# Two images through attention and a 3x3: the order at the seams and in the first image's last stage

## Chip, cores and metric

The kernel runs on one core of a Trainium2 chip. The metric is device time in microseconds (us), of which the medians of runs are compared. The engines are PE (matrix products), ACT (one-input functions, also reads products back from the accumulators), DVE (element-wise work and reductions), POOL (element-wise work, slower, and issues some DMAs) and SP (issues DMAs).

## The reference, cut to what matters

Two images of 256 channels and 64x64 pixels go through two layers. Both begin with a group normalisation and add their result to their input.

```python
# layer 0: x = x + attention(_gn(x)), 8 heads over all 4096 pixels
# layer 1: x = x + layer(_gn(x)):
q = _c1x1(x, conv1_w, conv1_b)
k = _c1x1(x, conv2_w, conv2_b)
v = _c1x1(x, conv3_w, conv3_b)
...
ctx = _sa(blockify(fq), blockify(fk), blockify(v), oh, ow)
feats = _bn_relu(_c1x1(ctx, lr_W_w), lr_W_scale, lr_W_shift)
feats = feats.reshape(b, DH, DW, C, oh, ow).transpose(0, 4, 5, 3, 1, 2).reshape(b * oh * ow, C, DH, DW)
qx = _bn_relu(_c1x1(_bn_relu(_c1x1(feats, sr_fq1_w), sr_fq1_scale, sr_fq1_shift), sr_fq2_w), sr_fq2_scale, sr_fq2_shift)
kx = _bn_relu(_c1x1(_bn_relu(_c1x1(feats, sr_fk1_w), sr_fk1_scale, sr_fk1_shift), sr_fk2_w), sr_fk2_scale, sr_fk2_shift)
vx = _c1x1(feats, sr_fv_w)
ctx2 = _sa(qx, kx, vx, DH, DW)
feats2 = _bn_relu(_c1x1(ctx2, sr_W_w), sr_W_scale, sr_W_shift)
out_att = feats2.reshape(b, oh, ow, C, DH, DW).transpose(0, 3, 1, 4, 2, 5).reshape(b, C, h, w)
...
f_all = jnp.einsum('bidn,oi->bodn', jnp.concatenate([qh, kh, vh], 1), fc_w)
f_conv = f_all.transpose(0, 2, 1, 3).reshape(b, hd * KC * KC, h, w)
out_conv = lax.conv_general_dilated(f_conv, dep_w, (1, 1), ((1, 1), (1, 1)), feature_group_count=hd, dimension_numbers=('NCHW', 'OIHW', 'NCHW'))
return rate1 * out_att + rate2 * out_conv
```

`_sa` is a softmax attention over 64 positions, once for each group of 64 pixels: first over pixels eight apart ("lr" in the kernel), then inside 8x8 blocks ("sr"). The last lines are linear in x, so the kernel computes them as one 3x3 convolution of the normalised picture, 256 to 256 channels, whose weights it works out on the chip from `conv1_w` to `conv3_w`, `fc_w` and `dep_w`.

## The kernel before

An image is eight tiles of 512 pixels (`NT` is 8), two partitions' worth of channels each (`KC` is 2): `xts[0]` to `xts[7]`. The loop over the two images `b` runs four stages one after the other.

- *Layer 0's start*: `group_stats` (bn_stats L326, bn_aggr L330, then `pm_l` L333 and `pv_l` L343, two tiny products that sum over a group's channels, with copies and a reciprocal on DVE and a root on ACT, L334 to L363, between and behind them), `normalise` (L368), and `project0`, whose first products are `p_wk` (L418).
- *Layer 0's attention* (to L652): from about 158 to 1150 us for image 0 and 1700 to 2745 us for image 1. Its sum is written back into the tiles (`put`, L652).
- *layer1_first* (from L1089). The seam: `to_groups(k, t, engine)` copies channel half k of tile t, normalised, into `xg` in another pixel order (L1102 on ACT, L1105 on DVE or POOL); `project(t, m, chunks)` multiplies `xg` into `py` (L1136), adds a position term (L1140, which reads `loc`, loaded by `open_pair` L1118) and copies it out (L1141). `st.means` and `st.variances` are `pm_l` and `pv_l` here. In image 0 a generator, `fold_products`, is stepped by `next(fold)` between these: it folds weights together on PE and copies them on ACT (`pt_fv` L263, `pm_fv` L269, `pb_lr` L278, copies L264 and L272, and L283 and L284 on DVE). Eight "lr" tiles of `group_attention` follow.
- *layer1_second* (from L1238): eight "sr" tiles, interleaved with the 3x3. A tile has a query branch (`branch`: `phq_sr` L1281, `prq_sr` L1289), a key branch (`phk_sr`, `prk_sr`), and `group_attention` in three parts: first values (`pvs_sr` L1013) and scores (`sp_sr` L1031) with a softmax on DVE and ACT (`nm_sr` L1045, `e_sr` L1047 and L1048, `den_sr` L1050 and L1051, `e_sr` L1052); then its transposition (`at_sr` L1057) and the other values; then `pc_sr` (L1075), read by ACT into `res`.

The 3x3 is sixteen steps, two tiles of the image (a strip) and a quarter of the work each, four steps to a strip. The picture `xp` is the normalised image with a border, made by `to_image(t)` on ACT (L1249, two instructions a tile). `conv_transform` turns it into `v` on POOL (one `col` L936, four `v` L940); the step ahead is always transformed. `conv_step` multiplies `v` and the weights `wf` (`mm` L950, 32 matmuls), and ACT (L955) and DVE (L956 to L977) add the result onto `xts`. `conv_edges` corrects the border (L984). When the four steps of a strip are done, its two tiles are finished: DVE adds `res` and `xts` (L1332), and SP writes the output (L1335).

For image 0 only, `conv_weights` makes the 3x3's weights on DVE from four loads, in two halves: 108 multiply-adds each (L870, L872), rows (L876 to L878), columns (L881 to L883), and SP writes them to a DRAM tile (L885). That takes DVE through the lr tiles and sr tile 0. `fetch_conv_weights` reads them back (L900, 4 MB); for image 0, PE transposes them (L909, 64 of them), ACT and DVE copy the results (L912, L914), and they are stored for image 1 (L915).

What sets the order: in the seam of layer1_first, PE, ACT and DVE run in the order of the text; in layer1_second only PE does, while a scheduler orders ACT, DVE and POOL from dependences, costs and priorities. SP issues its DMAs in order. In layer1_second the list `steps` says how many 3x3 steps a tile has: the first comes after the query branch, the second after the first part of the attention, the third after its end. Input tiles live in nine buffers, so the second image's tiles x_1_6 and x_1_7 are loaded (`load_x`, L70) only when outputs 5 and 6 of image 0 no longer need their inputs. The col buffer is one; `w4`, which holds `v` and most other intermediate tiles, has eleven.

Of the kernel before, what the change touches and what calls it, by code (L numbers as in the profile page):

```python
# [21 lines left out]
NT = N // T  # L22
KC = C // P
# [17 lines left out]
def direct_layers(ctx: ExitStack, tc: tile.TileContext, a: dict, out: bass.AP, bad: bass.AP):  # L41
# [3 lines left out]
    nc = tc.nc  # L45
# [1045 lines left out]
    def layer1_first(b, xts, put, check, st):  # L1091
# [6 lines left out]
        def to_groups(k, t, eng):  # L1098
            dst = xg[:, k, :, t, :].rearrange("p (d e) o -> p d e o", d=8)
            src = xts[t][:, k, :].rearrange("p (d o e) -> p d e o", d=8, o=8)  # L1100
            if eng is nc.scalar:
                return nc.scalar.activation(  # L1102
                    dst, src, AF.Identity, bias=shift[:, k : k + 1], scale=rstd[:, k : k + 1]
                )
            return eng.tensor_scalar(dst, src, mean[:, k : k + 1], rstd[:, k : k + 1], ALU.subtract, ALU.mult)  # L1105
# [10 lines left out]
        def open_pair(i):  # L1116
            loc = w4([16, 2, T], f"loc_{b}_{i}", F32R)
            nc.sync.dma_start(  # L1118
                out=loc.bitcast(F32).rearrange("r s n -> r (s n)"),
                in_=loc_kept[:, :, :, 2 * i * T : (2 * i + 2) * T].rearrange("l d r n -> (l d r) n"),  # L1120
            )
            locs[i] = loc
# [40 lines left out]
        with tc.manual_schedule(engines={E.PE, E.Activation, E.DVE}):  # L1163
            st.aggregate(second)
            fold = fold_products() if b == 0 else iter(())
            put(nc.gpsimd.tensor_copy, (0, 1))
            for t in range(5, NT):
                to_groups(0, t, nc.gpsimd)
            pm, pv = bank([P, 1], f"pm_l1_{b}"), bank([P, 1], f"pv_l1_{b}")
            to_groups(0, 0, nc.scalar)  # L1170
            next(fold, None)
            to_groups(0, 1, nc.scalar)
            next(fold, None)
            st.means(second, pm, nc.vector.tensor_copy)
            st.spread(second)
            to_groups(0, 2, nc.scalar)
            if b == 1:
                to_groups(0, 3, nc.scalar)
            next(fold, None)
            st.variances(second, pv)  # L1180
            st.deviations(second, pv)
            shift_of(st, 1)
            for _ in range(2):
                next(fold, None)
            for t in range(3 + b, 5):
                to_groups(0, t, nc.scalar)
            put(nc.scalar.copy, (2, 3))
            n_act = 2
            for t in range(NT):
                done = to_groups(1, t, nc.scalar if t < n_act else nc.vector)  # L1190
            for _ in fold:
                pass
            check()
            for i in range(2):
                open_pair(i)
            for t in range(2):
                for m in range(KC):
                    project(t, m, slice(0, 1))
            for t in range(2):
                for m in range(KC):  # L1200
                    project(t, m, slice(1, KC))
            at_grid(0)
        with tc.manual_schedule(engines={E.PE}):

            before = None
            for t in range(NT + 1):
                parts = None
                if t < NT:
                    def to_feats(m, pc, t=t):
# [6 lines left out]
                    parts = group_attention(  # L1216
                        f"lr_{b}_{t}", tiles.pop(t), source(t),
                        lambda c, w, t=t: source(t)[:, c, w * P : (w + 1) * P], wts["w3"], to_feats, b == 0,
                        more=(ats[rows, t // 4, :], grid[rows, :], t == 0),
                    )  # L1220
# [18 lines left out]
    def layer1_second(b, xts, feats, mean, rstd, shift, pacc):  # L1239

        xp = apool.tile([P, KC, PADW, PADW], F32, tag="A", name=f"xp_{b}")
        for k in range(KC):
            nc.gpsimd.memset(xp[:, k, 0, :], 0.0)
            nc.gpsimd.memset(xp[:, k, PADW - 1, :], 0.0)
            nc.gpsimd.memset(xp[:, k, 1 : PADW - 1, 0 : PADW : PADW - 1], 0.0)

        def to_image(t):
            for k in range(KC):
                nc.scalar.activation(  # L1249
                    xp[:, k, 1 + 8 * t : 9 + 8 * t, 1 : 1 + W], xts[t][:, k, :].rearrange("p (r w) -> p r w", w=W),  # L1250
                    AF.Identity, bias=shift[:, k : k + 1], scale=rstd[:, k : k + 1],
                )

        for t in range(3):
            to_image(t)
        results = {}
        turns = [divmod(n, 4) for n in range(4 * NT // 2)]
        ahead = {0: conv_transform(b, xp, *turns[0])}
        done = 0

        steps = (0, 0, 2, 3, 3, 3, 3, 2) if b == 0 else (3, 3, 2, 2, 2, 2, 2, 0)

        def conv():
            nonlocal done
            if done + 1 < len(turns):
                ahead[done + 1] = conv_transform(b, xp, *turns[done + 1])
            conv_step(b, xts, wf, ahead.pop(done), *turns[done], pacc)
            done += 1

        for t in range(NT):  # L1270
            nt = f"sr_{b}_{t}"
            f = [
                feats[k][:, 8 * t : 8 * t + 8].rearrange("p o d e -> p (o d e)") for k in range(KC)
            ]

            def branch(one, two, col1, col2, nm):
                hid = w4([P, KC, T], f"h{nm}_{nt}")
                for m in range(KC):
                    ph = bank([P, T], f"ph{nm}_{nt}_{m}")
                    for k in range(KC):  # L1280
                        nc.tensor.matmul(  # L1281
                            ph, wts[one][:, k, m * P : (m + 1) * P], f[k], start=k == 0, stop=k == KC - 1
                        )
                    bn_relu(hid[:, m, :], ph, col1, m)
                res = w4([P, KC, T], f"r{nm}_{nt}")
                pr = [bank([P, T], f"pr{nm}_{nt}_{m}") for m in range(KC)]
                for k in range(KC):
                    for m in range(KC):
                        nc.tensor.matmul(  # L1289
                            pr[m], wts[two][:, k, m * P : (m + 1) * P], hid[:, k, :], start=k == 0, stop=k == KC - 1  # L1290
                        )
                for m in range(KC):
                    bn_relu(res[:, m, :], pr[m], col2, m)
                return res

            with tc.manual_schedule(engines={mybir.EngineType.PE}):
                q = branch("fq1", "fq2", V_FQ1, V_FQ2, "q")
                for tt in {0: (3, 4)}.get(t, (t + 4,)):
                    if tt < NT:
                        to_image(tt)  # L1300
                if t == sum(n == 0 for n in steps[:-1]):
                    wf = fetch_conv_weights(b)
                if steps[t] > 0:
                    conv()
                k = branch("fk1", "fk2", V_FK1, V_FK2, "k")
                res = w4([P, KC, T], f"res_{nt}")

                def to_res(m, pc, res=res):

                    bn_relu(  # L1310
                        res[:, m, :].rearrange("p (d o e) -> p o d e", d=8, o=8),
                        pc.rearrange("p (o d e) -> p o d e", o=8, d=8), V_SRW, m,
                    )

                parts = group_attention(
                    nt, q, k, lambda c, w, f=f: f[c][:, w * P : (w + 1) * P], wts["fv"], to_res, apart=t + 1 < NT
                )
                next(parts)
                if steps[t] > 1:
                    conv()  # L1320
                next(parts)
                next(parts, None)
                if steps[t] > 2:
                    conv()
            conv_edges(xts, t)
            if b == B - 1 and t == 2:
                report()
            results[t] = res
            for n in sorted(n for n in results if done >= 4 * (n // 2 + 1)):
                res = results.pop(n)  # L1330
                for m in range(KC):
                    nc.vector.scalar_tensor_tensor(  # L1332
                        res[:, m, :], res[:, m, :], wts["rate1"], xts[n][:, m, :], ALU.mult, ALU.add
                    )
                nc.sync.dma_start(  # L1335
                    out=out[b, :, n * T : (n + 1) * T].rearrange("(k p) n -> p k n", p=P), in_=res
                )


    for b in range(B):  # L1340
        xts = x_first if b == 0 else load_x(b)
# [14 lines left out]
        with tc.tile_pool(name=f"sc_{b}", bufs=1, space=PSUM) as psum["sc"]:  # L1356
            put, check, st = attention0(b, xts, held)
# [565 lines left out]
```

## Time and profile before

| what | us |
|---|---|
| three runs | 3169.22, 3171.24, 3173.57 (median 3171.24) |
| profiled execution, its own time | 3168.58 |
| its span from first to last instruction | 3166.8 |
| mean granted TensorE clock | 0.989 |
| PE busy in the span | 3056.7 |
| DVE, ACT, POOL busy | 2467.7, 2304.5, 856.5 |

The profiled execution lies inside the runs' spread. A span of 3166.8 us with 1.8 us around it makes the execution's 3168.58. The page gives the span in 40 slices of 79 us: the digits are tenths of busy time, and in the row PEclk tenths of full clock. A row of a timeline has the start in us, the length in us, the engine, the line of the code, what is computed from what, how many such instructions it groups, and in brackets how long the engine stood idle before and what ended that. A row of windows has the stretch's limits and length, then busy time and number of instructions of PE, weight loads, DVE, ACT and POOL, the granted clock, the share of DMA time and GB/s. Image 0's stages of layer 1 lie from 1150 to 1600 us, image 1's from 2745 us to the end.

### The profile page before, as it was taken

The numbers are of one execution on the slowest core, as the hardware profiler recorded it, in microseconds if no ns is written. First come the engines' busy times: TensorE is split into PE (matmuls) and PEld (weight loads), VectorE is DVE, ScalarE is ACT, GpSimd is POOL, SyncE is SP. The second block draws the span as 40 slices with busy tenths as digits, with TensorE's granted clock in tenths as the row PEclk, the third lists the DMA queues.
The fourth block names the chain that finished last, engine by engine and source line by source line (L and its number), as shares of the span: only waits on it lengthen the run. The fifth ranks groups of instructions, "written<-read, shape, count | busy, mean of one in ns | idle before, by whom it ended". The sixth has DMA issues, their size and how long they took to land. (4 is left out here: it accounts for less than half of the span.)

```text
span 3166.8 us, 62680 instructions
## 1 busy us (share of the span) xinstructions
PE 3056.7 (97%) x25107; PEld 1832.7 (58%) x25107; DVE 2467.7 (78%) x3204; ACT 2304.5 (73%) x2359; POOL 856.5 (27%) x929
## 2 busy tenths in 40 slices
PE   7999999999999999799979999999999999899998
PEld 4455555555555546467755555555555555466766
DVE  4599999999999988745645999889999999824543
ACT  2699999999999973432225999999999999734232
POOL 2122222222222230435400222222222222305530
PEclk9999999999999999899989999999999999999999
DMA  7968779678796651211149696786878965600000
GB/s 249 276 127 171 152 160 182 135 171 171 162 191 127 140 127 52 83 54 54 40 163 276 131 185 141 154 175 144 171 168 164 186 145 125 161 1 8 21 14 22
DMA packets 242709, 425.74 MB, mean 134 GB/s; under 512 B 99164, under 2 KB 109984, under 8 KB 239976
## 3 DMA queue, kind: packets, MB, share of 16 engines
q0 software_dynamic: 96240, 240.41, 38.0%
q1 hardware_dynamic: 146168, 181.24, 20.3%
q8 instruction: 199, 3.26, 0.4%
q14 instruction: 102, 0.84, 0.1%
HBM read 118.52 MB, written 68.12 MB: 59 GB/s over the span
## 5 line engine op out<-in xcount | busy, mean ns | idle before, releaser
L564 DVE TENSOR_TENSOR e<-e,es 128x1024 f32<-128x1024 f32 (+1 forms) x952 | 1035.7, 1142 | 93.7 <-ACT es L517 91.7
L527 PE MATMUL av<-es,v 128*32 128x256 f32 (+1 forms) x9644 | 746.4, 390 | 0.0
L564 DVE TENSOR_TENSOR e<-e,v 128x1024 f32<-128x1024 f32 (+1 forms) x640 | 676.4, 1108 | 55.4 <-ACT v L517 54.0
L517 ACT ACTIVATE es<-sa 128x1536 f32<-128x1536 f32 (+1 forms) x444 | 635.9, 1432 | 95.3 <-PE sa L511 52.6
L511 PE MATMUL sa<-q,k 128*128 128x512 f32 x1736 | 560.9, 430 | 13.8 <-ACT es L517 6.6
L527 PE MATMUL av<-v 128*32 128x256 f32 (+1 forms) x6228 | 507.1, 390 | 0.0
L527 PEld LDWEIGHTS av<-es,v 128*32 128x32 f32 x9644 | 316.2, 109 | 299.5 <-issue 161.0
L511 PEld LDWEIGHTS sa<-q,k 128*128 128x128 f32 x1736 | 280.0, 188 | 296.0 <-issue 138.5
L511 PE MATMUL sc<-q,k 128*128 128x512 f32 x1180 | 371.5, 396 | 3.2 <-ACT es L517 2.1
L511 PE MATMUL sb<-q,k 128*128 128x512 f32 x1180 | 371.0, 395 | 0.0
L527 PEld LDWEIGHTS av<-v 128*32 128x32 f32 x6228 | 216.8, 110 | 179.2 <-issue 82.1
L517 ACT ACTIVATE es<-sc 128x1024 f32<-128x1024 f32 x296 | 306.4, 1035 | 1.7 <-DMA v<-es 1.7
L517 ACT ACTIVATE v<-sc 128x1024 f32<-128x1024 f32 x294 | 304.4, 1035 | 0.0
L517 ACT ACTIVATE es<-sb 128x1024 f32<-128x1024 f32 x296 | 302.0, 1020 | 0.7 <-DMA acc<-es 0.6
L517 ACT ACTIVATE v<-sb 128x1024 f32<-128x1024 f32 x294 | 300.0, 1020 | 0.0
L511 PEld LDWEIGHTS sc<-q,k 128*128 128x128 f32 x1180 | 210.0, 188 | 74.4 <-ACT es L517 13.5
L511 PEld LDWEIGHTS sb<-q,k 128*128 128x128 f32 x1180 | 221.2, 188 | 54.1 <-ACT es L517 1.6
L574 POOL DMA_DIRECT2D es<-es x118 | 100.7, 854 | 500.9 <-ACT es L517 436.6
L517 ACT ACTIVATE v<-sa 128x1536 f32<-128x1536 f32 (+1 forms) x146 | 209.3, 1434 | 35.5 <-PE sa L511 15.0
L950 PE MATMUL mm<-v,wf 128*128 128x256 f32 x1024 | 227.5, 380 | 0.0
L940 POOL TENSOR_TENSOR v<-col 128x512 f32<-128x512 f32 x128 | 161.5, 1289 | 238.8 <-PE mm L950 81.0
L950 PEld LDWEIGHTS mm<-v,wf 128*128 128x128 f32 x1024 | 193.5, 190 | 34.2 <-issue 8.6
(259 smaller groups left out, 3222.6 us busy)
## 6 DMA issues: line engine op xcount, KB each, us to landing
acc<-es POOLq DMA_DIRECT2D x130, 512.0 KB, 6.1
acc<-v POOLq DMA_DIRECT2D x84, 512.0 KB, 6.0
es<-es POOLq DMA_DIRECT2D x138, 256.0 KB, 4.1
v<-es POOLq DMA_DIRECT2D x134, 256.0 KB, 4.9
k<-wk_halves SPq DMA_DIRECT2D x64, 512.0 KB
q<-wq_halves SPq DMA_DIRECT2D x256, 128.0 KB
v<-v POOLq DMA_DIRECT2D x90, 256.0 KB, 4.8
es<-v POOLq DMA_DIRECT2D x86, 256.0 KB, 3.9
```

The source lines that it names most:

```text
L511: nc.tensor.matmul(sc[:, i, :], held["k", g // 2][:, j * P : (j + 1) * P], held["q", g, u // 2][:, u % 2, :], start=True, stop=True,)
L517: nc.scalar.activation(dst, sc[:, i : i + m, :], AF.Exp, scale=SC0)
L527: nc.tensor.matmul(dst[HD0 * u : HD0 * u + HD0, n], lhs, rhs(u)[:, n], start=start, stop=stop)
L564: nc.vector.tensor_add(dst[:, s, :], dst[:, s, :], src)
L574: nc.gpsimd.dma_start(out=dst, in_=src, accum_op=ALU.add)
L940: (nc.gpsimd.tensor_add if plus else nc.gpsimd.tensor_sub)(dst, rows(one), rows(two))
L950: nc.tensor.matmul(mm[:, m, r, :], wf[:, k, 4 * r + q, m * P : (m + 1) * P], v[r // 2][:, r % 2, k, :], start=k == 0, stop=k == KC - 1,)
```

## The change

At the seam into layer1_first, for both images: `open_pair` comes first; of the five copies of tiles 0 to 4 of the first channel half, which are ACT's, four (image 0) or five (image 1) now stand ahead of the means; image 0's folding pieces stand between them; x_6's and x_7's copies are given to POOL; in image 1 ACT takes three instead of two of the second half's copies, and one `project` half is issued between means and variances.

In layer1_second of image 0: steps (0, 0, 2, 3, 3, 3, 3, 2) become one in tile 1, after its first attention part, three in each of tiles 2 to 6, and none in tile 7. `to_image` and the first `conv_transform` are written in tiles 1 to 3 instead of ahead of the loop. The weights are fetched at the first step, in tile 1 after its scores, instead of in tile 2 after the query branch. Tile 0's second and third attention parts are kept back (`pending`) and issued after tile 1's query branch. The edges of tiles 0 and 1 are both added after tile 1. In image 1, `spots` and `images` give the same steps as before.

```diff
--- before.py
+++ after.py
@@ -1167,35 +1167,34 @@
             for t in range(5, NT):
                 to_groups(0, t, nc.gpsimd)
             pm, pv = bank([P, 1], f"pm_l1_{b}"), bank([P, 1], f"pv_l1_{b}")
-            to_groups(0, 0, nc.scalar)
-            next(fold, None)
-            to_groups(0, 1, nc.scalar)
-            next(fold, None)
+            for i in range(2):
+                open_pair(i)
+            for t in range(3):
+                to_groups(0, t, nc.scalar)
+                next(fold, None)
+            to_groups(0, 3, nc.scalar)
+            if b:
+                to_groups(0, 4, nc.scalar)
             st.means(second, pm, nc.vector.tensor_copy)
             st.spread(second)
-            to_groups(0, 2, nc.scalar)
-            if b == 1:
-                to_groups(0, 3, nc.scalar)
+            firsts = [lambda t=t, m=m: project(t, m, slice(0, 1)) for t in range(2) for m in range(KC)]
+            if b:
+                firsts.pop(0)()
             next(fold, None)
             st.variances(second, pv)
             st.deviations(second, pv)
             shift_of(st, 1)
-            for _ in range(2):
-                next(fold, None)
-            for t in range(3 + b, 5):
-                to_groups(0, t, nc.scalar)
-            put(nc.scalar.copy, (2, 3))
-            n_act = 2
+            if b == 0:
+                to_groups(0, 4, nc.scalar)
+            put(nc.gpsimd.tensor_copy, (2, 3))
+            n_act = 2 + b
             for t in range(NT):
                 done = to_groups(1, t, nc.scalar if t < n_act else nc.vector)
             for _ in fold:
                 pass
             check()
-            for i in range(2):
-                open_pair(i)
-            for t in range(2):
-                for m in range(KC):
-                    project(t, m, slice(0, 1))
+            for first in firsts:
+                first()
             for t in range(2):
                 for m in range(KC):
                     project(t, m, slice(1, KC))
@@ -1251,22 +1250,32 @@
                     AF.Identity, bias=shift[:, k : k + 1], scale=rstd[:, k : k + 1],
                 )
 
-        for t in range(3):
-            to_image(t)
         results = {}
         turns = [divmod(n, 4) for n in range(4 * NT // 2)]
-        ahead = {0: conv_transform(b, xp, *turns[0])}
+        ahead = {}
         done = 0
-
-        steps = (0, 0, 2, 3, 3, 3, 3, 2) if b == 0 else (3, 3, 2, 2, 2, 2, 2, 0)
+        wf = None
+
+
+        spots = {t: (0, 1, 2) for t in range(2, 7)} | {1: (1,)} if b == 0 else {
+            t: (0, 1, 2) if t < 2 else (0, 1) for t in range(NT - 1)
+        }
+        images = {1: range(5), 2: (5, 6), 3: (7,)} if b == 0 else {0: (3, 4), 1: (5,), 2: (6,), 3: (7,)}
 
         def conv():
-            nonlocal done
+            nonlocal done, wf
+            if wf is None:
+                wf = fetch_conv_weights(b)
             if done + 1 < len(turns):
                 ahead[done + 1] = conv_transform(b, xp, *turns[done + 1])
             conv_step(b, xts, wf, ahead.pop(done), *turns[done], pacc)
             done += 1
 
+        if b:
+            for t in range(3):
+                to_image(t)
+            ahead[0] = conv_transform(b, xp, *turns[0])
+        pending = None
         for t in range(NT):
             nt = f"sr_{b}_{t}"
             f = [
@@ -1295,12 +1304,15 @@
 
             with tc.manual_schedule(engines={mybir.EngineType.PE}):
                 q = branch("fq1", "fq2", V_FQ1, V_FQ2, "q")
-                for tt in {0: (3, 4)}.get(t, (t + 4,)):
-                    if tt < NT:
-                        to_image(tt)
-                if t == sum(n == 0 for n in steps[:-1]):
-                    wf = fetch_conv_weights(b)
-                if steps[t] > 0:
+                if pending:
+                    next(pending)
+                    next(pending, None)
+                    pending = None
+                for tt in images.get(t, ()):
+                    to_image(tt)
+                if b == 0 and t == 1:
+                    ahead[0] = conv_transform(b, xp, *turns[0])
+                if 0 in spots.get(t, ()):
                     conv()
                 k = branch("fk1", "fk2", V_FK1, V_FK2, "k")
                 res = w4([P, KC, T], f"res_{nt}")
@@ -1316,13 +1328,17 @@
                     nt, q, k, lambda c, w, f=f: f[c][:, w * P : (w + 1) * P], wts["fv"], to_res, apart=t + 1 < NT
                 )
                 next(parts)
-                if steps[t] > 1:
+                if 1 in spots.get(t, ()):
                     conv()
-                next(parts)
-                next(parts, None)
-                if steps[t] > 2:
+                if t == 0 and b == 0:
+                    pending = parts
+                else:
+                    next(parts)
+                    next(parts, None)
+                if 2 in spots.get(t, ()):
                     conv()
-            conv_edges(xts, t)
+            for tt in ((), (0, 1))[t] if b == 0 and t < 2 else (t,):
+                conv_edges(xts, tt)
             if b == B - 1 and t == 2:
                 report()
             results[t] = res
```

In the built program, as its order on each engine shows: on PE in image 0's seam `pt_fv` now precedes `pm_l` and `pm_fv` precedes `pv_l` (before: `pm_l`, `pt_fv`, `pv_l`, `pm_fv`), and on DVE six L1105 precede L283 and L284. In image 0's sr tile 0, ACT's sixteen L1249 stand where they stood before. DVE's L1050 to L1052 of tile 0 stand behind L876 to L883 of the second half of the weights (before: ahead of L876). POOL's second group of `v` waits for tile 0's `sp_sr` (before: for tile 1's `prq_sr` and `prk_sr`). At image 0's end, DVE's order is the sum L1332 of tile 6, statistics of x_1_7, tile 7's softmax, the sums of tile 7, and the copy of `pm_l`. In image 1's layer1_second all orders are as before.

## The prediction

> **What bounds the kernel now.** I read the page's busy times first, then its slices with the granted clock, then the waits, the windows around the two seams and the first image's 3x3, and last the timeline around each idle stretch of PE.
>
> ```profile
> PE 3056.7 (97%) x25107; PEld 1832.7 (58%) x25107; DVE 2467.7 (78%) x3204; ACT 2304.5 (73%) x2359; POOL 856.5 (27%) x929
> PE   7999999999999999799979999999999999899998
> PEclk9999999999999999899989999999999999999999
> 1267.00:1346.00 79.00, 58.83 (x296) 37.70 (x295) 61.54 (x156) 36.12 (x50) 31.81 (x15) 0.87 0.23 84
> 1583.00:1663.00 80.00, 63.18 (x246) 41.25 (x245) 36.12 (x76) 20.17 (x30) 0.70 (x1) 0.89 0.44 165
> PE pm_l L333 <- DVE mv_l L330: 37.6, 4, 17.0
> ```
>
> PE is the bound at 97%: what the change does not take out of PE's 110 us of idle time or out of its half-clock stretches does not shorten the run. The two windows are the change's places, with 20.2 and 16.8 us of PE idle. In the waits view `pm_l` behind `mv_l` costs 37.6 us in four places, the longest 17.0; three of them are at seams this change touches. The idle stretches between 1140 and 1640 us sum to 45.9 us. The rows that matter:
>
> ```profile
> 1289.46 20.07 POOL L936 TENSOR_TENSOR col<-xp 128x1152 f32<-128x1152 f32 x1 [7.05 <-ACT xp L1249]
> 1307.45 2.36 DVE L872 SCALAR_TENSOR_TENSOR prep<-prep 128x256 f32<-128x256 f32 x1
> 1309.61 5.50 POOL L940 TENSOR_TENSOR v<-col 128x512 f32<-128x512 f32 x4
> 1309.73 1.47 DVE L882 TENSOR_TENSOR prep<-prep 128x256 f32<-128x256 f32 x1
> 1320.63 0.69 PE L1057 MATMUL at_sr<-ident,e_sr 128*128 128x128 f32 x2 [11.65 <-DVE e_sr L1052]
> ...
> 1605.84 0.52 SPq L70 DMA_DIRECT2D x<-in_x_dram  x1
> 1609.82 1.29 DVE L326 BATCH_NORM_STATS2 stats_l<-x 128x6 f32<-128x512 f32 x2 [4.43 <-DMA x<-in_x_dram]
> 1611.75 0.56 PE L333 MATMUL pm_l<-mv_l,group 128*128 128x2 f32 x2 [11.17 <-DVE mv_l L330]
> 1616.28 16.62 PE L418 MATMUL p_wk<-xn,wqk 128*128 128x512 f32 x32 [2.55 <-DVE xn L368]
> ```
>
> The reader should see three stories. In tile 0 of the 3x3 stage PE waits 11.65 us for a softmax on DVE; DVE is not idle, it computes the 3x3's weights, and its instructions of 0.40 us (14 L872 take 5.62 us just before) take 1.47 to 2.36 us whenever POOL transforms the picture. At the end of image 0 PE waits 11.17 us, because the second image's last tile (`x_1_7`) is only loaded at 1605.84, after tile 7's output has freed a buffer. In the seam to layer 1 PE waits 1.46 us before `py` for ACT's copies, and its first products run at half clock.
>
> **What the Trainium skill says.** "SBUF — State Buffer", section "Who interferes with whom": a DVE instruction with two SBUF inputs contends with a GpSimd instruction that reads SBUF, the one that issues first holds the shared ports for its whole length, and "PE and ACT never wait on anyone". The trace agrees: L872 0.40 against 2.36 us next to `v`, and `col`, 2.20 us in its next use, held off 20.07 us by DVE's unbroken row of L872. "TensorE: Matmul & The Clock Gate", sections "What's actually happening" and "Why this matters for your kernels": PE falls to half rate after an idle window of about 3.4 us and needs as long a busy stretch to come back. In the trace the clock reads 0.5 at 1167.6 to 1177.9, 1311.0 to 1324.6, 1604.5 to 1621.6 and 2751.4 to 2765.0 us, each behind one of the gaps here; `py`'s matmuls there come every 0.85 us, later 0.43. So a removed gap also gives back up to half of the stretch behind it.
>
> **The change, part by part**, on the profiled execution's own clock (span 3166.8, with 1.8 us around it 3168.58; the median of the runs shown is 3171.24, so that execution lies 2.7 under it; I subtract from the median).
>
> *Image 0's seam to layer 1.* ACT's fourth copy of an input tile (L1102, 1.25 us) moves ahead of the means, the fifth stays behind L346, and two copies into x_6 and x_7 (L652, 0.63 each) leave ACT for POOL. The order of the built program also puts `pt_fv` ahead of `pm_l` and `pm_fv` ahead of `pv_l` on PE, and DVE's six L1105 (4.03 us) ahead of L283, which waits for PE's `pb_lr`. ACT finishes x_4 near 1169.8 instead of 1172.7; PE's first `py` follows: 1169.8 against 1172.81, -3.0. The second half needs DVE's six, now 1169.0 to 1173.1, in time for chunk two. Of the 10.2 us at half clock I claim 0.5 more. Gain 3.5, bounds 2 and 5. It carries over: DVE's weight program follows PE's lr tiles, since it waits for each tile's scores in its order and idles about 10 us in them.
>
> *Image 0: picture, transforms, tile 0's end.* The diff moves the pictures (`to_image`) to tile 1, and the first transforms with them. The built order says otherwise: ACT's sixteen L1249 keep their places in tile 0, and POOL's first `col` and `v` wait for the same things as before. Two things do change. POOL's second group of `v` waits only for tile 0's scores, not for tile 1's branches, so four `v` (1.05 us each, from 5.50 less its share of waits) and one more `col` (2.05) fall into DVE's weight work: about 6.2 us of blocking more. And the softmax's end (L1050 to L1052) stands behind the weights' rows and columns (L876 to L883), where it stood ahead of them. On PE, tile 0's end is put behind tile 1's query branch.
>
> Step by step: tile 0's scores end 3.5 early, 1305.5. Query branch of tile 1 on PE, 7.0 us, to 1312.6. DVE: the weight chain with the extra blocking lets `at_sr` start at about 1328.2 (before: 1320.63; +6.2 blocking, +5 rows and columns ahead, -3.5). Idle 15.5, against 11.65+2.94+2.56 = 17.15 for `at_sr_0`, `pc_sr_0` and `at_sr_1` together before. Then tile 0's rest 4.6, half clock 2.0, key branch 7.0, `pvs` and scores 3.0: PE is at the transposes of the weights at 1344.8. The weights' last write is issued about 5.3 us after L878 (12 writes at 0.44), 1329.9, read-back issued 1.8 later, 11 to 11.5 us long at 433 GB/s as before: 1343.2. So no wait, with 1.6 us to spare. Transposes 7.15 (row L909), first step 7.0, tile 1's end 4.3, tile 2's query branch 7.0: 1370.3, where PE had done this same work at 1375.5. Gain 5.2, of which 3.5 is the seam's: 1.7 for this part. Bounds: if the extra blocking doesn't happen, 13 more (softmax at 1316); if all of it is doubled, 6 less.
>
> *Tiles 2 to 7.* Fifteen steps in tiles 2 to 6 instead of fourteen; PE has no gap in either. Tile 7 has none now: its softmax (2.5 us on DVE) is covered by `pvs` (3.72), its last wait shrinks from 1.73 to about 1.2: 0.5.
>
> *Image 0's end.* The last step's matmuls now end about 23 us before tile 7's end instead of between its halves. Tile 6's sum (L1332) comes 7 us later, its output and the load of `x_1_7` are issued at +9, land at +13.4 (4.4 as before), statistics 1.3 and L330 0.6: +15.3, under tile 7's attention, which ends at +23. Queued behind these on DVE is tile 7's maximum (L1045), because the built order puts it after the statistics: its scores are ready at +15.6, so the wait costs nothing with about 1.5 us left. The 11.17 gap goes. Late next: the copy of `pm_l` (L334) stands behind tile 7's two L1332 on DVE, so from the end of tile 7 to `p_wk` I count 6.4 us (two L1332 after ACT's last output, copy, variance, first L368) against 11.17+4.5 = 15.7. Gain 9.3, bounds 6 and 11; the half clock behind it (1604.5 to 1621.6) shrinks: 1.0 more.
>
> *Image 1's seam.* ACT takes three of the eight second-half copies, DVE five, POOL the copies of x_6 and x_7, x_4 no longer waits for L346, and one `py` half fills the wait between `pm_l` and `pv_l`. The `py` block starts its second halves about 2763.6 instead of 2766.1: 2.3, bounds 1 and 3.5. `pm_l`'s own 6.77 stays. The rest of image 1 has the same order on every engine.
>
> Sum: 3.5+1.7+0.5+9.3+1.0+2.3 = 18.3. Span 3148.5, profiled 3150.3, median 3171.2-18.3 = 3152.9.
>
> **Rivals.** *A, transforms do not block* (DVE starves POOL, as in the 20.07 row, or the pictures do go behind the weights): `at_sr` of tile 0 has nothing to wait for, 13 us more: 3140. For: the 20.07; against: the order and the 1.47 rows, where POOL wins every second turn. *B, the end of image 0 gives nothing* (`x_1_7` or its statistics still last, for instance because tile 7's maximum waits behind them and pushes everything): 9 less: 3162. Against: 8 us between +15.3 and +23. *C, slower:* POOL and DVE lock each other for long. If the two `col` in tile 0 hold DVE 18 us each as one held POOL, the weights land 36 us later, and PE stands at the transposes in tile 1, since the step can no longer be preceded by tile 2's work; the cover there is 1.6 us. 36-1.6 = 34 lost less 18 won: 3187. It decides the sign from 20 us of delay. Against: no DVE row in the trace is held longer than 2.36. *D, it does nothing where it says*: the pictures stay in tile 0; that is in the forecast.
>
> **How the numbers follow.** Forecast 0.62, A 0.20, B 0.10, C 0.08. About 0.2%, 6.3 us, is what a measurement can tell from no change. Forecast's own range 3147 to 3159; A reaches to 3138, B to 3164; the range 3138 to 3163 leaves out C and the tails. Faster: forecast and A whole less 0.01 of tails, and 0.04 of B: 0.85. The other 0.06 of B falls within 0.2% (a seam that gives nothing goes with a tile 0 that gives less), with the 0.01: same 0.07. Slower is C: 0.08.
>
> **What would show it.** Right: `pm_l` of image 1's first stage with under 1 us of idle, `x_1_7` loaded before tile 7's scores; `at_sr_0` still waiting near 15 us, with L872 to L883 at 1.4 us beside `v`; L909 without a wait; `py` 3 us and 2 us earlier after its seams. Wrong: `at_sr_0` without a wait (A), an idle stretch ahead of L909 (C), or DVE's L1332 and L334 still late behind a load (B).

## The result and the profile after

The changed kernel took 3161.22 us (median of 7 runs, 3158.93 to 3165.79), the kernel before 3171.24 (7 runs, 3166.91 to 3173.57); the ratio is 0.9973, 95% interval 0.9961 to 0.9985. The medians differ by 10.0 us; the ratio, which is not that of the medians, stands for 8.6 us, its interval for 4.8 to 12.4. So 9 to 10 us were won where 18.3 were forecast.

The profiled execution (3162.76 us, span 3160.8) shows where. First the page's busy times and slices, in the same rows as before, then two windows of the same stretches, and three rows of PE's waits (total us, times, longest):

```profile
PE 3059.0 (97%) x25107; PEld 1835.6 (58%) x25107; DVE 2479.1 (78%) x3203; ACT 2302.7 (73%) x2356; POOL 864.9 (27%) x933
PE   7999999999999999799999999999999999999998
PEclk9999999999999999899999999999999999999999
```

```profile
1267.00:1346.00 79.00, 55.68 (x280) 35.22 (x277) 65.86 (x142) 34.55 (x48) 39.05 (x17) 0.85 0.20 72
1583.00:1663.00 80.00, 73.39 (x273) 45.67 (x272) 37.35 (x77) 25.41 (x37) 0.67 (x1) 0.98 0.53 187
```

```profile
PE pm_l L333 <- DVE mv_l L330: 25.5, 3, 16.5
PE at_sr L1057 <- DVE e_sr L1052: 17.7, 1, 17.7
...
PE mm L950 <- DVE z L959: 4.1, 1, 4.1
```

The second window, image 0's end, has gained 10.2 us of busy PE (63.18 to 73.39) and its clock rose from 0.89 to 0.98. The first, tile 0 of the 3x3 stage, has lost 3.2 (58.83 to 55.68): POOL works 7.2 us more there, and DVE 4.3. The waits say the same: `pm_l` fell from 37.6 us in four places to 25.5 in three, the wait for tile 0's softmax rose from 11.65 to 17.75, and a new row stands below, PE's `mm` waiting 4.1 us for DVE's L959.

PE's rows give the lengths of the stretches that the prediction had summed. All are counted from marks inside the same execution, so that layer 0's attention, which the change does not touch and which took 1.2 and 2.0 us longer in this execution, stays out.

| stretch (PE's rows) | before | after | won | forecast |
|---|---|---|---|---|
| end of attention to the end of the first step and all of tile 2's query branch | 216.8 | 215.4 | 1.4 | 5.2 |
| from there to tile 7's end | 225.1 | 230.9 | -5.8 | 0.5 |
| tile 7's end to the second image's `p_wk` | 15.7 | 5.4 | 10.3 | 9.3 |
| `p_wk` itself (half clock) | 16.6 | 15.6 | 1.0 | 1.0 |
| end of image 1's attention to the end | 409.7 | 407.0 | 2.7 | 2.3 |
| sum | | | 9.7 | 18.3 |

The end of the image and image 1's seam came as forecast. Two rows failed: the stretch to tile 2 kept 1.4 of 5.2, and the stretch of tiles 3 to 7, where no wait was expected, lost 5.8.

The timeline at image 0's end shows the part that held (here and below, selected rows):

```profile
1590.69 0.46 SPq L70 DMA_DIRECT2D x<-in_x_dram  x1
1594.92 1.28 DVE L326 BATCH_NORM_STATS2 stats_l<-x 128x6 f32<-128x512 f32 x2 [3.65 <-DMA x<-in_x_dram]
1597.67 1.03 PE L1031 MATMUL sp_sr<-rk_sr,rq_sr 128*64 128x64 f32 x28 [0.46 <-ACT rk_sr L1086]
1606.96 0.38 PE L333 MATMUL pm_l<-mv_l,group 128*128 128x2 f32 x2 [0.87 <-ACT res_sr L1086]
1607.72 0.16 DVE L334 COPY mean_l<-pm_l 128x2 f32<-128x2 f32 x1
1611.44 4.01 PE L418 MATMUL p_wk<-xn,wqk 128*128 128x512 f32 x5 [2.54 <-DVE xn L368]
```

The load of x_1_7 is issued before tile 7's scores and its statistics are done before tile 7's softmax begins, so `pm_l` waits 0.87 instead of 11.17 us. Of `p_wk` 3.3 us still run at half clock, before 5.3: that is the 1.0 in the table.

The timeline one tile and a half earlier shows the new wait. DVE's queue is to be read from top to bottom:

```profile
1538.21 0.68 DVE L956 TENSOR_TENSOR z<-z,mm 128x512 f32<-128x512 f32 x1
1538.75 1.26 SPq L70 DMA_DIRECT2D x<-in_x_dram  x2
1543.44 0.69 DVE L326 BATCH_NORM_STATS2 stats_l<-x 128x6 f32<-128x512 f32 x1 [4.55 <-DMA x<-in_x_dram]
1544.05 0.67 DVE L957 TENSOR_TENSOR z<-z,mm 128x512 f32<-128x512 f32 x1
1545.49 0.68 DVE L959 TENSOR_TENSOR z<-z,mm 128x512 f32<-128x512 f32 x1
1546.32 1.94 PE L950 MATMUL mm<-v,wf 128*128 128x256 f32 x4 [4.15 <-DVE z L959]
```

Between two additions of one 3x3 step, DVE stands 4.55 us at the statistics of x_1_5, whose load was only issued at 1538.75. L957 to L959 of that step are queued behind it, and PE's next step needs the accumulator that they read. That step then takes 8.83 us instead of 7.07, for its first part runs at half clock (0.5 for 3.4 us from 1546.4). In the kernel before, the same loads were issued 7.1 us later, counted from the end of the attention, and these statistics stood behind tile 6's softmax, where they waited 0.85 us and PE waited for nothing:

```profile
1544.71 1.29 SPq L70 DMA_DIRECT2D x<-in_x_dram  x2
1547.34 1.24 DVE L1052 TENSOR_TENSOR e_sr<-e_sr,den_sr 128x256 f32<-128x256 f32 x1
1549.43 2.55 DVE L326 BATCH_NORM_STATS2 stats_l<-x 128x6 f32<-128x512 f32 x4 [0.85 <-DMA x<-in_x_dram]
```

Last, tile 0, DVE's and POOL's rows and the wait that they end in:

```profile
1288.88 22.44 POOL L936 TENSOR_TENSOR col<-xp 128x1152 f32<-128x1152 f32 x1 [7.05 <-ACT xp L1248]
1309.25 2.36 DVE L872 SCALAR_TENSOR_TENSOR prep<-prep 128x256 f32<-128x256 f32 x1
1317.25 0.42 DVE L1045 TENSOR_REDUCE nm_sr<-sp_sr 128x4 f32<-128x256 f32 x1
1319.29 5.31 POOL L940 TENSOR_TENSOR v<-col 128x512 f32<-128x512 f32 x4
1321.94 1.55 DVE L872 SCALAR_TENSOR_TENSOR prep<-prep 128x256 f32<-128x256 f32 x1
1324.68 2.78 POOL L936 TENSOR_TENSOR col<-xp 128x1152 f32<-128x1152 f32 x1
1325.41 2.33 DVE L881 TENSOR_TENSOR prep<-prep 128x256 f32<-128x256 f32 x1
1331.07 1.09 DVE L883 TENSOR_TENSOR prep<-prep 128x256 f32<-128x256 f32 x3
1332.74 0.42 DVE L1052 TENSOR_TENSOR e_sr<-e_sr,den_sr 128x256 f32<-128x256 f32 x1
1333.22 0.69 PE L1057 MATMUL at_sr<-ident,e_sr 128*128 128x128 f32 x2 [17.75 <-DVE e_sr L1052]
```

The second group of `v` and one `col` more run into DVE's weights, and L1052 comes behind the weights' last columns (L883).

### The profile page after: what moved, and what is told of

The parts are those of the page before. It is cut to its first block, busy times and chain, and to the rows that moved or that the text cites. A ratio compares the mean times of both kernels' runs of the same rounds, so it can differ in the third digit from the quotient of the medians.

```text
span 3160.8 us, 62690 instructions
## 1 busy us (share of the span) xinstructions
PE 3059.0 (97%) x25107; PEld 1835.6 (58%) x25107; DVE 2479.1 (78%) x3203; ACT 2302.7 (73%) x2356; POOL 864.9 (27%) x933
## 5 line engine op out<-in xcount | busy, mean ns | idle before, releaser
L950 PE MATMUL mm<-v,wf 128*128 128x256 f32 x1024 | 229.3, 383 | 4.1 <-DVE z L959 4.1
L950 PEld LDWEIGHTS mm<-v,wf 128*128 128x128 f32 x1024 | 194.9, 191 | 39.4 <-issue 13.5
```

What stands on the lines that cost most here:

```text
L950: nc.tensor.matmul(mm[:, m, r, :], wf[:, k, 4 * r + q, m * P : (m + 1) * P], v[r // 2][:, r % 2, k, :], start=k == 0, stop=k == KC - 1,)
```

## The experiments

Each kernel ran beside the kernel before on one chip; a ratio is to that. On the three chips the kernel before had medians of 3169.99, 3170.41 and 3170.88 us. A trace is one execution, so its marks and the medians need not agree. Where a mark of PE is given in us, it is counted from the end of image 0's attention in the same execution.

**Statistics of x_1_5 and x_1_6 behind tile 6's softmax.** Only these four instructions of DVE move; `kept["late"]` is tile 6's L1052.

```diff
+            if late and t in (5, 6):
+                with tc.issue_after(late.ins):
+                    for k in range(KC):
+                        st.tile(k, t)
+                continue
```

> The changed kernel, with the statistics of the second image's tiles x_1_5 and x_1_6 (L326 on DVE) queued behind tile 6's softmax; nothing else moves. Theory 'queue': in the changed kernel DVE stands 4.55 us at the statistics of x_1_5, waiting for its load, with the subtraction L957 of the 3x3's step 12 queued behind; PE's step 13 needs that accumulator. Then step 13 starts without its 4.15 us wait and takes 7.1 instead of 8.83 us, image 0 ends 5.9 us earlier, and the run is about 5.9 us shorter than the changed kernel's 3161. Rival 'DVE late anyway': POOL's transforms hold DVE back at that place (L1348 at 1.75 us, two L984 at 2.46), so a wait of 3 us or more stays before step 13 and the time does not move. Second rival: the four statistics, now later, put the load or statistics of x_1_7 last again, and 'pm_l' waits several us more.

3153.91 us (5 runs), ratio 0.9949 (0.9936 to 0.9962). The timeline, in which the lines of the code are two to eleven further on (L957 is the matmul L950, L963 to L966 are L956 to L959):

```profile
1528.36 1.75 DVE L1359 SCALAR_TENSOR_TENSOR res_sr<-res_sr,rate,x 128x512 f32<-128x512 f32 x1
1536.81 1.26 SPq L70 DMA_DIRECT2D x<-in_x_dram  x2
1536.98 0.69 DVE L964 TENSOR_TENSOR z<-z,mm 128x512 f32<-128x512 f32 x1
1538.44 0.68 DVE L966 TENSOR_TENSOR z<-z,mm 128x512 f32<-128x512 f32 x1
1540.10 7.07 PE L957 MATMUL mm<-v,wf 128*128 128x256 f32 x32
...
1559.26 2.46 DVE L328 BATCH_NORM_STATS2 stats_l<-x 128x6 f32<-128x512 f32 x4
```

DVE goes straight from one addition to the next, PE's step starts without a wait and takes 7.07 us, and the first statistics follow 20 us later without one. POOL still holds DVE up ahead of it (L1359, the sum, at 1.75 us), so that was not the cause. From the attention's end to `p_wk` it is 445.25 us against 451.60: 6.35 won. The rival of a late DVE falls, and so does the second: `pm_l` keeps its 0.87. The table's second stretch, to tile 7's end, takes 224.8 us in all four traces with these statistics late; in the six others with the changed steps or the last one put back, PE waits 3.9 to 4.2 us ahead of this step and the stretch takes 230.6 to 232.2.

**The last step back in tile 7**, the rest as changed:

```diff
-        spots = {t: (0, 1, 2) for t in range(2, 7)} | {1: (1,)} if b == 0 else {
+        spots = {t: (0, 1, 2) for t in range(2, 6)} | {1: (1,), 6: (0, 1), 7: (1,)} if b == 0 else {
```

> The changed kernel with only the last 3x3 step of image 0 put back into tile 7, behind its scores, as before the change. This measures the end of image 0 by itself. Theory: outputs 6 and 7 and the load of x_1_7 come last again, 'pm_l' waits 11 us, and the 10.4 us between tile 7's end and p_wk come back: about 10.5 to 11.5 us longer than the changed kernel, 3172, no better than the kernel before. Rival: the load is early enough anyway, since tile 6 holds a step more than before; then less than 5 us are lost.

3173.4 us (13 runs), ratio 1.0007 (0.9999 to 1.0015). The end of image 0 again:

```profile
1610.69 0.51 SPq L70 DMA_DIRECT2D x<-in_x_dram  x1
1615.06 1.29 DVE L326 BATCH_NORM_STATS2 stats_l<-x 128x6 f32<-128x512 f32 x2 [4.82 <-DMA x<-in_x_dram]
1616.99 0.56 PE L333 MATMUL pm_l<-mv_l,group 128*128 128x2 f32 x2 [11.56 <-DVE mv_l L330]
```

The 11 us are back (16.1 us from tile 7's end to `p_wk`, against 5.4), and the whole gain is gone: all other parts of the change together came to nothing.

**The seams of before in the changed kernel:**

> The changed kernel with both seams into layer 1 written as before; steps, pictures and tile 0's end as changed. Theory from the two traces: the seams give 1.8 us in image 0 and 2.7 in image 1, so this run is 4.5 us longer than the changed kernel, about 3165.7. The prediction had 3.5 and 2.3, 5.8 in all. Rival: the seam's gain in image 0 is lost in tile 0, where PE waits for DVE's weights anyway, unless DVE's weights move with it; then only the 2.7 of image 1 is missing.

3161.0 us (8 runs), ratio 0.9973 (0.9963 to 0.9983). By PE's rows the first `py` comes 2.3 us later than in the changed kernel and tile 0 begins 1.8 later, but the first 3x3 step comes at 197.48 us against 197.39: the rival's case. Image 1's stage took 4.8 us longer in this execution, 3.2 of it before its sr tiles; the other 1.6 fell in code that is the same, and two more executions showed 1.6 there. That was not explained. The medians, 3161.0 and the changed kernel's 3161.22, do not show the 2.7 us of image 1's seam; their intervals, 3 to 4 us to each side, are too wide to tell.

**The seams alone**, in the kernel before:

> The kernel before with both seams into layer 1 as changed, and nothing else. Its built order shows a side effect in image 0: DVE's reciprocal and L1052 of tile 0's softmax fall behind the rows and columns of the weights, far from the seam. Theory 'order': PE reaches tile 0 two to three us earlier, but waits 4 us or more longer for the softmax (11.65 before), so by the first 3x3 step nothing is left of image 0's seam or a little is lost; image 1 gains its 2.7; about 3168. Rival 'carries', the prediction's: the weights' work on DVE starts earlier too and image 0 keeps 3.5, 6 in all: 3164.5.

3167.85 us (21 runs), ratio 0.9992 (0.9986 to 0.9999). Tile 0's rows of DVE and PE:

```profile
1314.09 0.40 DVE L1050 TENSOR_REDUCE den_sr<-e_sr 128x4 f32<-128x256 f32 x1
1314.42 0.94 DVE L876 TENSOR_TENSOR prep<-prep 128x768 f32<-128x768 f32 x1
...
1319.04 1.08 DVE L883 TENSOR_TENSOR prep<-prep 128x256 f32<-128x256 f32 x3
...
1320.24 0.42 DVE L1052 TENSOR_TENSOR e_sr<-e_sr,den_sr 128x256 f32<-128x256 f32 x1
1320.72 0.69 PE L1057 MATMUL at_sr<-ident,e_sr 128*128 128x128 f32 x2 [18.85 <-DVE e_sr L1052]
```

Tile 0 begins 4.6 us earlier (127.24 against 131.82), and PE then waits 18.85 us where the two waits of before were 11.65 and 2.94. The first 3x3 step comes at 209.72, before at 209.91. The edit to the seam has changed DVE's order in tile 0, 110 us away: the reciprocal and L1052 now stand behind twelve instructions for rows and columns. The weights themselves are done earlier, at 163.99 against 168.09, so DVE's work did follow PE; the softmax, now behind it, did not. What is left is image 1's 2.7 us; the medians differ by 3.0.

**Transforms behind the weights.** A one-column copy on POOL that reads the last column of the weights is put ahead of the first `col`; the orders of all other engines are the same.

```diff
+        gate = const.tile([P, 1], F32, name="gate")
+        kept["gate"] = nc.gpsimd.tensor_copy(gate, new_cols[:, 3, 1, 0:1])
...
+                    with tc.issue_after(kept["gate"].ins):
+                        ahead[0] = conv_transform(b, xp, *turns[0])
```

> The changed kernel, with a one-column copy on POOL that reads the last of the 3x3's weights put ahead of POOL's first col: picture and transforms really stand behind the weights. Theory 'lock': beside col and v, DVE's instructions of tile 0 take 13.5 us more than alone (7.8 as before the change, 5.7 new). Then L872 to L883 stay at 0.4 us, PE's wait for tile 0's softmax falls from 17.75 to about 4.5 us, the weights land 13 us earlier too, and the run is 12 to 13 us shorter than the changed kernel: about 3148.5. Rival 'weights last': the writes and the read-back do not follow, PE then waits ahead of the 64 transpositions, and the run gains 5 us at most. Rival 'transforms last': the first v are ready after the weights, PE waits at the first step for POOL, gain below 8.

3161.6 us as a median of 22 runs, from 3152.99 to 3173.05; ratio 0.9975 (0.9968 to 0.9982). The trace shows the gain, 184.41 us to the first step against 197.39, and the median does not. Neither rival came: PE's longest wait ahead of the transpositions is 0.74 us, and at the first step it does not wait for POOL. So a second kernel has the copy go to a dead part of the weights' buffer:

```diff
+        kept["gate"] = nc.gpsimd.tensor_copy(tmp[:, 0, 0, 0:1], new_cols[:, 3, 1, 0:1])
```

> As the kernel with late transforms, but the one-column copy on POOL writes into a dead part of the weights' own buffer instead of a tile of its own; all orders are the same. In the run before, image 0 up to the first 3x3 step was 13 us shorter than in the changed kernel by its trace (184.4 against 197.4 us from the end of the attention), yet the median of 22 runs was no better than the changed kernel's and they spread over 20 us, with both attention stages 3 us longer. Theory 'place': the extra tile moves the buffers behind it, and the attention stages, which the edit does not touch, run slower for it. Then this run has a spread under 9 us and a median of 3148 to 3149. Rival 'order': late transforms themselves make the times spread, and this run is near 3161 again.

3152.05 us (5 runs, 3148.14 to 3159.41), ratio 0.9944 (0.9930 to 0.9958). The spread is 11 us, not under 9, and the median 3 above what was expected; by the trace the first step comes at 185.53. The two stretches to the end of each image's attention took 1158.7 and 1135.4 us in this execution, with the extra tile 1161.5 and 1137.0, in the kernel before 1158.7 and 1133.0. In the other ten traces they lie between 1156.1 and 1159.9 and between 1132.5 and 1135.0, and the kernels with and without the tile ran on two chips; that the tile's place slows them is not shown. The rows of tile 0 (the code's later lines are one further on):

```profile
1306.41 0.47 DVE L872 SCALAR_TENSOR_TENSOR prep<-prep 128x256 f32<-128x256 f32 x1
1306.81 0.41 DVE L882 TENSOR_TENSOR prep<-prep 128x256 f32<-128x256 f32 x1
...
1315.12 1.09 DVE L883 TENSOR_TENSOR prep<-prep 128x256 f32<-128x256 f32 x3
1316.22 2.13 POOL L937 TENSOR_TENSOR col<-xp 128x1152 f32<-128x1152 f32 x1
...
1320.04 0.69 PE L1058 MATMUL at_sr<-ident,e_sr 128*128 128x128 f32 x2 [9.11 <-DVE e_sr L1053]
```

L872 and L882 take 0.47 and 0.41 us, where they took 1.47 beside `v`; the weights' 283 DVE instructions take 126.1 us in all, before 133.8, after 137.0. The last of them ends at 157.5 us after the attention, before 168.1, after 172.3. This is the lock between POOL and DVE, priced: 10.9 us of the changed kernel's DVE time on the weights, and 11.9 us at the first 3x3 step.

**The softmax's end ahead of the weights' rows**, in the changed kernel; `conv_weights` stops before the second half's rows and goes on behind tile 0's L1052:

```diff
+                if b == 0 and t == 0:
+                    with tc.issue_after(kept["soft"].ins):
+                        next(kept["weights"], None)
```

> The changed kernel, with the end of tile 0's softmax (L1050 to L1052) ahead of the rows and columns of the second half of the weights, where it stood before the change; POOL's transforms as in the changed kernel. The softmax is then ready some 5 to 7 us earlier and PE's wait of 17.75 us falls to 11 to 13. Theory 'weights next': the weights are not earlier, PE reaches the transpositions 5 to 6 us earlier and waits there for the read-back, so the time gains 1 us at most. Rival 'softmax is the bound': nothing waits there, and the run is 5 us shorter than the changed kernel.

3158.3 us (5 runs), ratio 0.9962 (0.9949 to 0.9975). Between the two theories: the first 3x3 step comes 3.1 us earlier (194.26). In place of the wait of 17.75 us stand three: 4.5 us for the softmax, 10.5 for DVE's copy of `at_sr`, which now stands behind the rows, and 1.75 ahead of the transpositions.

**Both losses undone, and then the softmax too:**

> Both single edits together: statistics of x_1_5 and x_1_6 behind tile 6's softmax, transforms behind the weights (without a tile of their own). If the two losses are independent the gains add: 6.4 and 13 us by the traces, about 3142. Rival: with image 0 further ahead another wait takes over (weights' read-back, or the load of x_1_7) and less than 16 of the 19.4 us come.

3149.15 us (5 runs, 3141.95 to 3153.72), ratio 0.9934 (0.9920 to 0.9947). By PE's rows `p_wk` comes at 434.10 us, 17.5 earlier than in the changed kernel; the single edits gave 6.35 and 10.8, so they add. The median shows 12.1 of it; the profiled execution (3141.95) is the fastest of the five.

> The kernel before in this list, and tile 0's softmax end ahead of the weights' rows and columns. In the run with the softmax first alone the wait split in two (4.5 us for the softmax, 10.5 us for the copy of at_sr, which then stood behind the weights on DVE) and 1.75 us at the transpositions; 3.1 us were gained by the first 3x3 step. Theory 'weights next': with the transforms late, PE reaches the transpositions when the weights land, so putting the softmax first gains under 1.5 us over the kernel with the two edits. Rival: 3 us again.

3140.42 us (4 runs, 3140.35 to 3142.92), ratio 0.9905 (0.9890 to 0.9920): the best median, 20.8 us under the changed kernel. By PE's rows it is only 0.6 us better than the one before it (433.48), so 'weights next' holds, and the rest of the 8.7 us between their medians is in layer 0's attention or in the scatter of few runs (the two profiled executions took 3141.95 and 3142.92). PE's waits that are left there, for DVE's copy of `at_sr` and ahead of the transpositions (L1089 is L1075, L920 is L909):

```profile
1319.90 3.75 PE L1089 MATMUL pc_sr<-bd,vs_sr 128*128 128x128 f32 x16 [4.80 <-DVE bd L1080]
...
1335.27 1.97 PE L920 MATMUL pw<-ident,wf 128*128 128x128 f32 x16 [0.74 <-DMA wf<-wf_kept]
```

**The kernel with both losses undone, with the seams of before:**

> The kernel with statistics and transforms late, with both seams as before the change. Theory 'order': the first 3x3 step comes within 1.5 us of where it came with the changed seams (186.0 us after the attention), though the first py is 3 us later, since the softmax's end stands ahead of the weights' rows again; only image 1's 2.7 is lost. Rival 'carries': with no transforms to hold DVE, the seam's gain in image 0 arrives, and the first step comes 3 us later without it, 5.7 lost in all.

3149.0 us (6 runs), ratio 0.9935 (0.9922 to 0.9948). The first step comes at 184.69 us, with the changed seams at 185.98. So image 0's seam is worth nothing here either; `p_wk` comes at 432.90, the earliest of all. Image 1 takes 2.9 us longer, and the medians (3149.15 with the changed seams) do not show it.

PE's marks together, us from the end of image 0's attention; the last column is the length of image 1 from the end of its attention:

| kernel | first `py` | tile 0 begins | first step | `p_wk` | image 1 |
|---|---|---|---|---|---|
| before | 14.13 | 131.82 | 209.91 | 457.61 | 409.70 |
| changed | 11.89 | 130.06 | 197.39 | 451.60 | 407.01 |
| statistics late | 11.69 | 129.35 | 197.12 | 445.25 | 406.99 |
| transforms late, own tile | 10.83 | 127.24 | 184.41 | 439.68 | 408.60 |
| transforms late, no tile | 11.30 | 128.35 | 185.53 | 440.79 | 407.02 |
| softmax first | 11.24 | 128.57 | 194.26 | 448.42 | 406.98 |
| last step back | 10.82 | 128.92 | 196.02 | 462.35 | 408.61 |
| seams of before | 14.15 | 131.82 | 197.48 | 451.74 | 411.82 |
| seams alone | 10.83 | 127.24 | 209.72 | 457.88 | 407.02 |
| statistics and transforms late | 10.83 | 128.83 | 185.98 | 434.10 | 406.98 |
| and softmax first | 11.90 | 131.51 | 185.35 | 433.48 | 407.00 |
| both late, seams of before | 14.35 | 131.04 | 184.69 | 432.90 | 409.94 |

The first step is not at the same place in the work in all kernels: in the two rows that keep the old steps (before, seams alone) tile 2's query branch lies ahead of it.

## Why the prediction was right and wrong

- *The number:* 3161.2 lies inside the stated range and beside rival B's 3162, but not for B's reason. B had the end of image 0 give nothing, and it gave the most; what is missing from the forecast was lost in two other places, named below. That the sum fell near B's is luck.
- *Which way, and the end of image 0:* right. 9.3 was forecast for the stretch to `p_wk`, 10.3 came; the half clock behind it gave the 1.0. With the last step back, 12 us are lost by the medians, more than the whole net gain.
- *Image 1's seam:* right, 2.7 against 2.3. In all nine traces with the changed seam image 1's first sr tile begins 126.4 us after its attention, in the three without at 129.1 to 129.6.
- *"PE has no gap in either" (tiles 2 to 7): the step that failed most*, by 6.3 us. I had followed x_1_7 through DVE's order and asked what stands behind its statistics, but not x_1_5 and x_1_6, which the same edit had moved: with three steps in tiles 2 to 6 the third strip is done a tile earlier, outputs 4 and 5 go out earlier, and the loads they set free land in the middle of another step. The scheduler put the first of their statistics between two additions. Moving four instructions gave 6.35 us back, so this is shown.
- *"It carries over: DVE's weight program follows PE's lr tiles":* the second step that failed, by some 3.8 us with what hangs on it. The seam itself had about the right size for PE, 3.0 forecast for the first `py` and 2.2 to 3.3 in the nine traces that have the changed seam. In the changed kernel 1.75 us of the 3.5 are left at the end of tile 0's scores, and the wait for the softmax is 17.75 us instead of 15.5. Two terms of that wait were mis-sized. The weights' last row ends 4.2 us later than before (172.3 us after the attention against 168.1), where 6.2 less 3.5, so 2.7, were forecast. And the softmax ends 1.0 us behind that row instead of 6.2 ahead of it: the order cost 7.2 us, where 5 were forecast. With the seams alone the weights do end 4.1 us earlier, and PE still waits longer, for the softmax now ends behind them. In all three comparisons of seams nothing of image 0's seam reaches the first 3x3 step. The order of the softmax is not the whole reason: where it stands ahead of the rows in both (185.35 us with the changed seams, 184.69 with those of before), the gain is gone when tile 0 begins (131.51 and 131.04). How much reaches tile 0 differs from trace to trace, 0.3 to 4.6 us against the kernel before; why stays open.
- *POOL's extra transforms in tile 0:* the size was right. 6.2 us of blocking were forecast; the five lengthened rows behind the maximum (1.14, 1.22, 1.55, 1.22 and 2.33 us against 0.47, 0.22, 0.47, 0.20 and 0.42) hold 5.7 us more. One row had been misread: the L872 of 2.36 us stands beside the end of `col` (to 1309.53), not beside `v` (from 1309.61).
- *Rival A*, no blocking at all, had put its gain at 13 us. It did not happen, but making it happen gave its price: 11.9 at the first step. The two col rows of rival C lasted 2.2 and 2.8 us, with no long lock of DVE.
- With the four statistics moved, the changed kernel takes 3153.9, near the forecast: 16.1 us under the kernel before that ran beside it. The 2.2 to the forecast's 18.3 are about the 3.8 that did not carry, less 1.4 that the end of image 0 and image 1's seam gave above it.

## What to carry to other kernels

When work is moved to an earlier place, list every load that its finished outputs release, and for each find the first instruction that waits for it and what is queued behind that instruction; one early consumer in an in-order queue can cost the wait for its load and more (here 4.15 us and 6.35 in all). It need not: in the kernel before, DVE waited 4.91 us for a load up to 1493.2, and PE, which had a key branch to do there, lost nothing. A gain at a seam counts only at the next place where PE does not wait for another engine, so carry it forward to there before adding it. And where a scheduler makes the order, compare the orders for each part of an edit alone: here the seam's edit reordered a softmax 110 us later.

## What the runs showed of the hardware

DVE and POOL hold each other up by a multiple of their own time: a 0.4 us instruction took 1.47 beside `v`, and POOL's `col`, 2.1 us where it ran behind the weights, lasted 22.4 us beside an unbroken row of DVE instructions in the changed kernel. The wait of PE that the early statistics caused, 3.9 to 4.2 us in six traces, also slowed the step behind it: it took 8.83 to 10.17 us there, and 7.07 without the wait.
